# One transformer block on one core: the second norm, the second-half residuals and the shared-expert sums change engines

## The chip, the core and the metric

The kernel runs on one NeuronCore of one Trainium2 chip. The metric is the device time of one execution, in microseconds (us). Engines are named as the profile names them: PE multiplies matrices (PEld are its weight loads), DVE is the vector engine, ACT the scalar engine, POOL is GpSimd, SP issues the DMAs; "q" behind a name means the queue of that engine. All data are float32.

## The reference, cut to what matters

```python
# x: 4 batches of 512 tokens of width 512;  sa, ca, ga, sb, cb, gb: one row of 512 per batch
gb = (2 * (gb >= 0) - 1) * jnp.maximum(jnp.abs(gb), 0.25)      # ga likewise: never near zero
h = layernorm(x) * (1 + ca) + sa
x = x + ga * attention(h)                                      # 16 heads of 128, causal
h = layernorm(x) * (1 + cb) + sb                               # "the second norm"
x = x + gb * ffn(h)
# ffn(h) = shared(h) + sum over the top 2 of 8 experts of weight * expert(h)
# shared and expert are both silu(h @ wg.T) * (h @ wu.T) @ wd.T
```

Three pieces concern us: the second norm, the residual `x + gb * (shared + w1*y1 + w2*y2)`, and the shared expert's down projection.

## The kernel before

**Stages.** Attention runs over the four batches in turn, up to about 1270 us of the span; the second norm of a batch and its routing (`second_norm`, L943) are slipped into the attention of the following batch. For the last batch they are slipped into the first half of the shared expert instead. Then come: the shared expert for batches 0 and 1 ("half 1", about 1270 to 1389 us), 39 tiles of 128 routed tokens through their experts (about 1389 to 1709 us, results to `ys` in DRAM), and the shared expert for batches 2 and 3 ("half 2", from 1709 us), beside which the routed results of all 16 blocks of tokens are gathered and added by `combine`.

**Products.** Every large matrix product is done as seven products of quadrants in place of eight (`seven`, L510). A product fills one of three PSUM banks `w`, and DVE or ACT empties it; so PE can run two to three products ahead of DVE before it must wait. For this, sums and differences of the quadrants are needed: `hidden_sums` (L1274) makes four of them of the hidden values that feed the down projection of a batch, on DVE for the first batch of a half (n = 0), on POOL for the second (n = 1). `shared_down` (L1291) takes the seven products of the down projection and adds them, times gb, to the residual `xres`: DVE adds the two terms into `sy` and multiplies by gb (L1330 to L1333), POOL adds that to the residual (L1318). In the very last product (`last`, L1336) the two terms are multiplied by gb and added one by one, the last add on DVE.

**Second norm.** `normed` (L210): the statistics on DVE (L226, L227), a reciprocal root on ACT as Ln and Exp (L232, L233), then for each of four blocks of 128 tokens: `xh = src*rstd + less` on ACT (L251), times a row on DVE (L258), plus a row on POOL (L259). `less` is a small DVE operation right behind the Exp (L236). The four blocks are then transposed by PE (L267, tile `pln`) for the router. In the first norm (n = 1) one DVE operation (L242) does the subtraction and the scaling.

**Order.** The order on PE, DVE, ACT and SP is the order of the program text: generators that yield after each step are woven by hand (`weave`, `weave_at`), and an engine takes its instructions strictly in that order. POOL's order is left to a scheduler. `combine` (L1506) advances twice per block of tokens: ACT multiplies y1 by its weight, then DVE does `y2*w2 + y1` (L1511) and the product with gb (L1514), and POOL adds to the residual (L1515). The blocks of tokens come in the order of batches 0, 2, 3, 1; batches 0 and 1 are written out from `combine` (`finish`), batches 2 and 3 from `shared_down`.

Of the kernel before, what the change touches and what calls it, by code (L numbers as in the profile page):

```python
# [14 lines left out]
P = 128  # L15
# [16 lines left out]
FK = 3  # L32
# [16 lines left out]
def adaln_block_kernel(  # L49
# [160 lines left out]
    def normed(b, n, fine=(1,)):  # L210


        if n == 1:
            src = xh = late["first"]
        else:
            src = xres[b]
            xh = late["x"]
            rows = late["mod"]
            for t in range(NTB):
                nc.vector.tensor_mul(src[:, t, :], src[:, t, :], ga_bc)  # L220
                nc.gpsimd.tensor_add(src[:, t, :], src[:, t, :], xh[:, t, :])
                yield
        mv = small.tile([P, NTB, 2], F32, tag="mv", name=f"mv_{n}_{b}")
        for t in range(NTB):
            st = small.tile([P, 6], F32, tag="st", name=f"st_{n}_{b}_{t}")
            nc.vector.bn_stats(st, src[:, t, :])  # L226
            nc.vector.bn_aggr(mv[:, t, :], st)  # L227
            if t in fine:
                yield
        rstd = small.tile([P, NTB], F32, tag="rstd", name=f"rstd_{n}_{b}")  # L230
        nc.vector.tensor_scalar_add(rstd, mv[:, :, 1], EPS)
        nc.scalar.activation(rstd, rstd, AF.Ln)  # L232
        nc.scalar.activation(rstd, rstd, AF.Exp, scale=-0.5)  # L233
        if n == 2:
            less = small.tile([P, NTB], F32, tag="less", name=f"less_{n}_{b}")
            nc.vector.scalar_tensor_tensor(  # L236
                less, mv[:, :, 0], -1.0, rstd, op0=ALU.mult, op1=ALU.mult
            )
        yield
        for t in range(NTB):  # L240
            if n == 1:
                nc.vector.tensor_scalar(  # L242
                    xh[:, t, :],
                    src[:, t, :],
                    mv[:, t, 0:1],
                    rstd[:, t : t + 1],
                    op0=ALU.subtract,
                    op1=ALU.mult,
                )
            else:  # L250
                nc.scalar.activation(  # L251
                    xh[:, t, :],
                    src[:, t, :],
                    AF.Identity,
                    bias=less[:, t : t + 1],
                    scale=rstd[:, t : t + 1],
                )
                nc.vector.tensor_mul(xh[:, t, :], xh[:, t, :], rows[0])  # L258
                nc.gpsimd.tensor_add(xh[:, t, :], xh[:, t, :], rows[1])  # L259
            if t in fine:  # L260
                yield
        late[b] = xh
# [414 lines left out]
    def halves(a):  # L677
        return a.rearrange("p (t n) -> p t n", t=2)
# [592 lines left out]
            rows = slice(kh * FT, (kh + 1) * FT)  # L1271
            nc.vector.tensor_mul(hid[:FT, :, kh::2, 1, :], g[rows], u[rows])

    def hidden_sums(b, n, cs):  # L1274

        if n == 1:
            place = flat_of(h2s[b + 1])
            places = [place[:, q * FK * HW : (q + 1) * FK * HW] for q in range(3)]
        else:
            x1, x2 = wdn if b == 0 else [flat_of(w) for w in ws[:2]]  # L1280
            places = [x1[:, : FK * HW], x1[:, FK * HW : 2 * FK * HW], x2[:, : FK * HW]]
        s4, s5, s6 = (q.rearrange("p (c n) -> p c n", c=FK) for q in places)
        eng = nc.gpsimd if n else nc.vector
        a = hids[b][:, n]
        eng.tensor_add(s4[:, cs], a[:, 2, cs], a[:, 3, cs])
        eng.tensor_sub(s5[:, cs], s4[:, cs], a[:, 0, cs])
        eng.tensor_sub(a[:, 2, cs], a[:, 0, cs], a[:, 2, cs])
        eng.tensor_sub(s6[:, cs], a[:, 1, cs], s5[:, cs])
        return [a[:, q] for q in range(4)] + [s4, s5, s6]

    def shared_down(b, n, slots7):  # L1291

        bn = b + n

        def mm(i, dst):
            sa, sb_ = PROD[i]
            for t2 in range(2):
                for c in range(FK):
                    rows = FL if c == 1 else P
                    nc.tensor.matmul(  # L1300
                        dst[:, t2 * HW : (t2 + 1) * HW],
                        lhsT=slots7[sa][:rows, c, t2 * P : (t2 + 1) * P],
                        rhs=sdn[:rows, sb_, c, :],
                        start=(t2 == 0 and c == 0),
                        stop=(t2 == 1 and c == FK - 1),
                    )

        def gb(s):
            return gb_bc[:, bn, s * HW : (s + 1) * HW].unsqueeze(1).to_broadcast([P, 2, HW])

        def sy():
            return halves(work.tile([P, D], F32, tag="gy", name=f"sy_{bn}"))

        def into(r, s):
            return xres[bn][:, 2 * r : 2 * r + 2, s * HW : (s + 1) * HW]

        def done(r, s, y, eng=nc.gpsimd):
            eng.tensor_add(into(r, s), into(r, s), y)  # L1318
            if b >= half:
                nc.sync.dma_start(  # L1320
                    out=out[bn, r * HW : (r + 1) * HW, s * HW : (s + 1) * HW].rearrange(
                        "(t p) n -> p t n", p=P
                    ),
                    in_=into(r, s),
                )

        def add(p, u, r, s, less=False):
            y = sy()
            if less:
                nc.vector.tensor_sub(y, halves(u), halves(p))  # L1330
            else:
                nc.vector.tensor_add(y, halves(p), halves(u))
            nc.vector.tensor_mul(y, y, gb(s))  # L1333
            done(r, s, y)

        def last(p, u4):  # L1336
            if (b, n) != (half, 1):
                return add(p, u4, 0, 1)
            y = sy()
            nc.vector.tensor_mul(y, halves(p), gb(1))  # L1340
            done(0, 1, y, nc.vector)

        def less(p, u3):
            add(p, u3, 1, 0, True)
            if (b, n) == (half, 1):

                u4 = halves(places["p1"])
                nc.vector.tensor_mul(u4, u4, gb(1))
                nc.gpsimd.tensor_add(into(0, 1), into(0, 1), u4)

        places = {
            key: flat_of(h2s[b])[:, q * S : (q + 1) * S] for q, key in enumerate(("p1", "u2", "u3"))
        }
        yield from seven(
            f"d_{bn}",
            S,
            mm,
            {
                "p1": lambda o, p: nc.scalar.copy(o, p),
                "u2": lambda o, p, u: nc.vector.tensor_add(o, p, u),  # L1360
                "11": lambda p, p1: add(p, p1, 0, 0),
                "u3": lambda o, p, u: nc.vector.tensor_add(o, p, u),
                "22": lambda p, u3: add(p, u3, 1, 1),
                "u4": lambda o, p, u: nc.vector.tensor_add(o, p, u),
                "21": less,
                "12": last,
            },
            places,
        )

    def shared(b):

        for k in range(NSC):
            for n, _ in enumerate(in_order(shared_hidden(b, k))):
                if n == 0 and k > 0:
                    keep_hidden(b, k - 1)
                if n == 2 and k == NSC - 1:
                    hidden_sums(b, 0, slice(0, 2))
                yield
        keep_hidden(b, NSC - 1)  # L1380
        slots7 = hidden_sums(b, 0, slice(2, 3))
        more = hidden_sums(b, 1, slice(0, 3))
        yield from in_order(shared_down(b, 0, slots7))
        yield from in_order(shared_down(b, 1, more))

    NSEV = NSC * SEVEN
# [118 lines left out]

    def combine(n, bt):  # L1506
        b, t = divmod(bt, NTB)
        y1, y2 = (y_sb[n][:, k, :] for k in range(TOPK))
        nc.scalar.mul(y1, y1, cw[0][:, bt : bt + 1])
        yield  # L1510
        nc.vector.scalar_tensor_tensor(  # L1511
            y2, y2, cw[1][:, bt : bt + 1], y1, op0=ALU.mult, op1=ALU.add
        )
        nc.vector.tensor_mul(y2, y2, gb_bc[:, b, :])  # L1514
        nc.gpsimd.tensor_add(xres[b][:, t, :], xres[b][:, t, :], y2)  # L1515
        if b < half:
            finish(bt)

    with tc.manual_schedule(engines={ENG.PE, ENG.DVE, ENG.Activation, ENG.SP}):
        load_h2(0)  # L1520
# [52 lines left out]
            nc.sync.dma_start(out=xr[b], in_=xres[b].rearrange("p t d -> p (t d)"))  # L1573
        open_phase("tiles")
        turned = {0: tile_in(0, xts.pop(0))}
        flat, made = {}, {}
        for i in range(NT + 1):
            if i < NT:
                ht = tile_hidden(i, turned.pop(i))
# [13 lines left out]
            if i == 4:  # L1593
                load_h2(2)
                load_h2(3)
            if i == 8:
                most_of_b(nc.gpsimd, h2s[2])
                most_of_b(nc.gpsimd, h2s[3])
# [2 lines left out]
        open_phase("half2")  # L1601
        order = [bt for b in (0, 2, 3, 1) for bt in range(b * NTB, (b + 1) * NTB)]
        open_hidden(2)
        load_xr(2, moe, "xr0")
        load_xr(0, moe, "xr1")
        shared_tail(2)
        shared_tail(3)
# [134 lines left out]
```

## Time and profile before

| | |
|---|---|
| median of 3 runs | 1827.33 us (1825.96 to 1829.34) |
| the profiled execution: its own time | 1831.47 us |
| its span in the profile | 1829.8 us, 21973 instructions |
| PE busy | 1741.7 us (95%) |
| DVE busy | 884.8 us (48%) |
| POOL busy | 628.3 us (34%) |
| ACT busy | 562.7 us (31%) |
| mean granted PE clock | 0.983 |

The span is the stretch of the profile in which the engines work; the execution's own time holds 1.7 us more around it. Busy shares are means over stages that are very different: in the tile stage DVE is busy a fifth of the time, in half 2 nearly always. PE being "busy" includes matmuls that take twice as long because the granted clock is half, so the clock has to be read beside it.

### The profile page before, as it was taken

The page shows a single profiled execution, that of the slowest core. Times are in us where ns is not written, and L with a number is a line of the kernel's source. Part 1 is how long each engine was busy: PE and PEld are TensorE (multiplying, and loading weights), DVE is VectorE, ACT ScalarE, POOL GpSimd, SP SyncE. Part 2 cuts the span into 40 slices and gives each one's busy share as a digit, 9 for nine tenths or more (in the row PEclk, how much of TensorE's full clock was granted, in tenths as well). Part 3 has the DMA queues.
Part 4 walks back from the last instruction along what each step waited for, and adds up shares of the span by engine and source line. Part 5 has one row for each costly group of instructions (what it writes and reads, how often), then busy time and mean ns, then how long its engine had stood idle before and what let it go on. Part 6 is the DMA issues. An engine that isn't in the chain of part 4 may idle for free.

```text
span 1829.8 us, 21973 instructions
## 1 busy us (share of the span) xinstructions
PE 1741.7 (95%) x7637; PEld 1326.9 (73%) x7637; DVE 884.8 (48%) x1860; ACT 562.7 (31%) x1341; POOL 628.3 (34%) x726
## 2 busy tenths in 40 slices
PE   6999999997999999799999989999999999999997
PEld 4767778785887788678778767886786565565676
DVE  4554454455455555554654645444683211111497
ACT  1034443205445412534441354443310111111220
POOL 6344662305153312443331446435241100000475
PEclk9999999999999999899999989999999999999999
DMA  6569899545342243434243366436142656554442
GB/s 247 178 207 307 254 303 299 196 155 182 101 150 101 83 159 121 150 107 144 81 142 121 121 225 202 123 116 243 44 153 101 224 179 223 168 193 136 143 122 98
DMA packets 157838, 301.93 MB, mean 165 GB/s; under 512 B 19216, under 2 KB 97552, under 8 KB 151072
## 3 DMA queue, kind: packets, MB, share of 16 engines
q1 hardware_dynamic: 152608, 283.75, 46.3%
q0 software_dynamic: 5120, 16.78, 2.8%
q8 instruction: 61, 1.00, 0.2%
q14 instruction: 49, 0.40, 0.1%
HBM read 254.72 MB, written 97.03 MB: 192 GB/s over the span
## 4 chain that ended last, share of the span: by engine, by line
PE 79%; DVE 7%; POOL 5%; ACT 3%; DMA 3%; issue 2%; SPq 0%; POOLq 0%; ACTq 0%; DVEq 0%
PE w_v L687 10%; PE w_q L601 10%; PE w_o L724 9%; PE w_k L639 7%; PE ps L776 6%; PE po L818 6%; PE pyt L1469 5%; PE pgt L1442 5%; PE put L1442 5%; PE w_s L1227 4%; PE w_d L1300 4%; PE ppt L804 3%; ACT prob L794 1%; PE pxt L1429 1%; DMA xt<-xs 1%
## 5 line engine op out<-in xcount | busy, mean ns | idle before, releaser
L787 ACT ACTIVATE prob<-ps,nmax 128x128 f32<-128x128 f32 (+3 forms) x256 | 134.1, 524 | 371.7 <-DVE nmax L785 371.7
L639 PE MATMUL w_k<-h,wk 128*128 128x256 f32 x896 | 226.2, 391 | 4.8 <-DVE h L495 2.6
L724 PE MATMUL w_o<-wo,oS 128*128 128x256 f32 x896 | 208.9, 379 | 0.0
L687 PE MATMUL w_v<-wv,h 128*128 128x256 f32 x896 | 206.1, 379 | 2.0 <-DVE u_q L621 1.2
L601 PE MATMUL w_q<-h,wq 128*128 128x256 f32 x896 | 204.6, 383 | 1.3 <-DVE qT L627 1.3
L601 PEld LDWEIGHTS w_q<-h,wq 128*128 128x128 f32 x896 | 170.7, 192 | 28.0 <-issue 3.4
L639 PEld LDWEIGHTS w_k<-h,wk 128*128 128x128 f32 x896 | 168.3, 197 | 28.2 <-ACT p_k L651 4.8
L687 PEld LDWEIGHTS w_v<-wv,h 128*128 128x128 f32 x896 | 167.3, 190 | 23.9 <-DVE u_q L621 1.6
L724 PEld LDWEIGHTS w_o<-wo,oS 128*128 128x128 f32 x896 | 164.6, 190 | 21.3 <-issue 1.4
L776 PE MATMUL ps<-kT,qT 128*128 128x128 f32 (+3 forms) x512 | 177.0, 449 | 1.4 <-ACT prob L787 1.4
L818 PE MATMUL po<-probT,v 128*128 128x512 f32 (+3 forms) x512 | 153.5, 440 | 18.7 <-DVE probT L812 18.6
L818 PEld LDWEIGHTS po<-probT,v 128*128 128x128 f32 x512 | 96.1, 192 | 77.2 <-issue 30.3
L794 ACT ACTIVATE prob<-prob,rsum 128x128 f32<-128x128 f32 (+3 forms) x256 | 122.8, 551 | 55.7 <-DVE rsum L791 55.7
L804 PEld LDWEIGHTS ppt<-ident,prob 128*128 128x128 f32 x640 | 84.2, 144 | 74.4 <-issue 38.1
L1227 PE MATMUL w_s<-h2s,ws 128*128 128x256 f32 x560 | 126.1, 382 | 7.7 <-DVE wgu L1254 2.6
L737 POOL TENSOR_TENSOR xres<-xres,p_o 128x512 f32<-128x512 f32 x48 | 60.9, 1268 | 211.0 <-DVE xres L737 118.8
L785 DVE TENSOR_REDUCE nmax<-ps 128x1 f32<-128x128 f32 (+3 forms) x256 | 125.8, 491 | 8.8
L1227 PEld LDWEIGHTS w_s<-h2s,ws 128*128 128x128 f32 x560 | 104.7, 190 | 27.2 <-DVE wgu L1254 3.8
L804 PE MATMUL ppt<-ident,prob 128*128 128x128 f32 x640 | 108.9, 280 | 7.7 <-ACT prob L794 4.9
L783 DVE TENSOR_TENSOR ps<-ps,cmask 128x128 f32<-128x128 f32 x256 | 75.2, 294 | 70.6 <-PE ps L776 62.1
L1469 PE MATMUL pyt<-wdn,hTt 128*128 128x512 f32 (+1 forms) x234 | 107.0, 593 | 0.6 <-ACT yt L1477 0.6
L1452 DVE TENSOR_TENSOR ht<-tsg,put 128x352 f32<-128x352 f32 x39 | 20.3, 521 | 170.4 <-PE put L1442 165.6
(271 smaller groups left out, 2443.8 us busy)
## 6 DMA issues: line engine op xcount, KB each, us to landing
wgu<-in_wexp_dram SPq DMA_DIRECT2D x39, 1408.0 KB, 8.6
xs<-nothing SPq DMA_DIRECT2D x15, 2304.0 KB, 15.7
wdn<-in_wexp_dram SPq DMA_DIRECT2D x39, 768.0 KB, 4.4
wo<-sums_o SPq DMA_DIRECT2D x12, 1536.0 KB, 7.7
wq<-sums_q SPq DMA_DIRECT2D x24, 640.0 KB, 4.7
wk<-sums_k SPq DMA_DIRECT2D x24, 640.0 KB, 4.6
wv<-sums_v SPq DMA_DIRECT2D x12, 1280.0 KB, 7.1
xt<-xs SPq DMA_DIRECT2D x39, 256.0 KB, 2.9
```

Of the source, the lines that this page charges most:

```text
L601: nc.tensor.matmul(dst, lhsT=w[:, sa, c, :], rhs=h7[b][:, sb_, c, :], start=c == 0, stop=c == 1,)
L639: nc.tensor.matmul(dst, lhsT=w[:, sa, c, :], rhs=h7[b][:, sb_, c, :], start=c == 0, stop=c == 1,)
L687: nc.tensor.matmul(dst[:, t2 * HW : (t2 + 1) * HW], lhsT=h7[b][:, sb_, c, t2 * P : (t2 + 1) * P], rhs=w[:, sa, c, :], start=t2 == 0 and c ...
L724: nc.tensor.matmul(dst[:, t2 * HW : (t2 + 1) * HW], lhsT=oSs[hp][:, sa, t2 * P : (t2 + 1) * P], rhs=w[:, hp, sb_, :], start=t2 == 0 and hp ...
L776: nc.tensor.matmul(ps[:, :n], lhsT=qT[:, q0 : q0 + P], rhs=kT[:, u % 2, :n], start=True, stop=True,)
L787: nc.scalar.activation(blk, ps[:, :n], AF.Exp, bias=nmax, accum_out=rsum[:, i : i + 1])
L794: nc.scalar.mul(blk, blk, rsum[:, k : k + 1])
L804: nc.tensor.transpose(pt[:, at : at + P], prob[:, QO[i] + j * P : QO[i] + (j + 1) * P], ident,)
L818: nc.tensor.matmul(po[:, j * P :], lhsT=v()[:, j, u * DH : (u + 1) * DH], rhs=probT[:, KO[j] : KO[j] + (NTB - j) * P], start=(j == 0), sto ...
L1227: nc.tensor.matmul(dst[:, n * HW : (n + 1) * HW], lhsT=ws[k][:, sa, c, :], rhs=h2s[b + n][:, sb_, c, :], start=(n == 0 and c == 0), stop=( ...
L1442: nc.tensor.matmul(ps[:, :F], lhsT=xT[:, c, :], rhs=wgu[i % 2][:, at : at + F], start=(c == 0), stop=(c == NC - 1),)
L1469: nc.tensor.matmul(py, lhsT=hT_t[:fn, k, :], rhs=wdn[i % 2][:fn, k * D : (k + 1) * D], start=(k == 0), stop=(k == len(FCH) - 1),)
```

## The change

- **Second norm.** In batches 0, 1 and 2 the subtraction and scaling go from ACT to one DVE operation with two per-token scalars, as in the first norm; `less` is no longer made there. Only the last batch keeps the ACT form. The DVE product with a row and the POOL sum stay.
- **Residuals of batches 2 and 3.** During the tile stage, from tile 6 on, `divided` loads the residual of batch 2 (this load was at the start of half 2), makes 1/gb for the two batches in eight pieces of 128 columns on DVE, and multiplies the eight residual blocks by it on POOL, one step per tile. `combine` for these batches is then two DVE operations `x = y*w + x`; `shared_down` adds both terms into the residual and multiplies the finished block by gb, all on DVE.
- **Residuals of batches 0 and 1** in `shared_down`: the add into the residual goes from POOL to DVE.
- **hidden_sums** is a generator, always on DVE. The first two thirds for n = 0 are taken one operation after each of four products of the fifth piece (before: all four together); those for n = 1 one after each of four products of the first batch's down projection (before: POOL).

```diff
@@ normed
+        idle = n == 2 and b == B - 1
+        if idle:
             less = small.tile(...)
...
         for t in range(NTB):
-            if n == 1:
+            if not idle:
                 nc.vector.tensor_scalar(xh[:, t, :], src[:, t, :], mv[:, t, 0:1], rstd[:, t : t + 1], ...)
             else:
                 nc.scalar.activation(xh[:, t, :], src[:, t, :], AF.Identity, bias=less..., scale=rstd...)
+            if n == 2:
                 nc.vector.tensor_mul(xh[:, t, :], xh[:, t, :], rows[0])
                 nc.gpsimd.tensor_add(xh[:, t, :], xh[:, t, :], rows[1])
@@ hidden_sums
-        eng = nc.gpsimd if n else nc.vector
-        eng.tensor_add(s4[:, cs], a[:, 2, cs], a[:, 3, cs])
-        eng.tensor_sub(s5[:, cs], s4[:, cs], a[:, 0, cs])
-        eng.tensor_sub(a[:, 2, cs], a[:, 0, cs], a[:, 2, cs])
-        eng.tensor_sub(s6[:, cs], a[:, 1, cs], s5[:, cs])
+    def hidden_sums(slots7, cs):
+        a11, a12, a21, a22, s4, s5, s6 = (a[:, cs] for a in slots7)
+        nc.vector.tensor_add(s4, a21, a22)
+        yield
+        nc.vector.tensor_sub(s5, s4, a11)
+        yield
+        nc.vector.tensor_sub(a21, a11, a21)
+        yield
+        nc.vector.tensor_sub(s6, a12, s5)
+        yield
@@ shared_down
+        def add(r, s, *terms, sub=None):
             if b >= half:
+                if sub is not None:
+                    nc.vector.tensor_sub(into(r, s), into(r, s), halves(sub))
+                for a in terms:
+                    nc.vector.tensor_add(into(r, s), into(r, s), halves(a))
+                nc.vector.tensor_mul(into(r, s), into(r, s), gb(s))
                 nc.sync.dma_start(out=..., in_=into(r, s))
+                return
             y = sy()
             ...                                   # y = the two terms, as before
             nc.vector.tensor_mul(y, y, gb(s))
-            done(r, s, y)                         # POOL: into += y
+            nc.vector.tensor_add(into(r, s), into(r, s), y)
+        def u4(o, p, u2):
+            nc.vector.tensor_add(o, p, u2)
+            if b >= half:
+                nc.vector.tensor_add(into(0, 1), into(0, 1), halves(o))
         def last(p, u4):
-            if (b, n) != (half, 1):
-                return add(p, u4, 0, 1)
-            ...
+            add(0, 1, p, *(() if b >= half else (u4,)))
@@ shared
+        sums7 = hidden_sums(slots7, slice(0, 2))
-                if n == 2 and k == NSC - 1:
-                    hidden_sums(b, 0, slice(0, 2))
+                if 0 < n < 5 and k == NSC - 1:
+                    next(sums7)
...
-        more = hidden_sums(b, 1, slice(0, 3))
-        yield from in_order(shared_down(b, 0, slots7))
+        for n, _ in enumerate(in_order(shared_down(b, 0, slots7))):
+            if 1 < n < 6:
+                next(sums7)                       # the sums of batch b + 1
+            yield
@@ combine
+        if b >= half:
+            nc.vector.scalar_tensor_tensor(x_t, y1, w1, x_t, op0=ALU.mult, op1=ALU.add)
+            yield
+            nc.vector.scalar_tensor_tensor(x_t, y2, w2, x_t, op0=ALU.mult, op1=ALU.add)
+            return
...
+    def divided():
+        load_xr(2, moe, "xr0")
+        rgb = phase[-1].tile([P, 2, D], F32, tag="rgb", bufs=1, name="rgb")
+        for n in range(2):
+            for c in range(NC):
+                cols = slice(c * P, (c + 1) * P)
+                nc.vector.reciprocal(rgb[:, n, cols], gb_bc[:, half + n, cols])
+                yield
+        for b in range(half, B):
+            for t in range(NTB):
+                nc.gpsimd.tensor_mul(xres[b][:, t, :], xres[b][:, t, :], rgb[:, b - half, :])
+                yield
@@ tile loop
+            if i >= 6:
+                next(ready, None)
...
-        load_xr(2, moe, "xr0")
```

## The prediction, made before the changed kernel was run

> **What bounds the kernel now.** I read the chain that ended last, then the list of what PE waited for, then the timeline and the windows around the longest waits. The chain first (shares of the span by engine), then PE's waits (total us, times, longest):
>
> ```profile
> PE 79%; DVE 7%; POOL 5%; ACT 3%; DMA 3%; issue 2%; SPq 0%; POOLq 0%; ACTq 0%; DVEq 0%
> ```
> ```profile
> PE po L818 <- DVE probT L812: 18.6, 8, 4.0
> PE pln L267 <- POOL xh L259: 15.2, 6, 4.3
> ...
> PE w_s L1227 <- DVE wgu L1254: 2.6, 1, 2.6
> ```
>
> PE is the bound, so only its waits and its clock are worth anything. The two large waits lie in one place: the second norm of batches 0, 1 and 2. Asked by window (425:475, 735:785, 1040:1090 us), PE waits 3.7, 3.7, 4.0 us for `probT` and 5.2, 5.1, 4.8 us for `xh`. The timeline of batch 0 (start, length, engine, line, what, and in brackets the idle time before it and who ended it):
>
> ```profile
> 441.36 0.17 DVE L236 SCALAR_TENSOR_TENSOR less<-mv,rstd 128x4 f32<-128x4 f32 x1 [1.99 <-ACT rstd L233]
> ...
> 442.97 1.11 PE L818 MATMUL po<-probT,v 128*128 128x256 f32 x4 [3.70 <-DVE probT L812]
> ...
> 448.45 0.73 POOL L486 TENSOR_TENSOR oS<-oS 128x256 f32<-128x256 f32 x1 [0.34 <-ACT oS L825]
> ...
> 449.11 1.82 DVE L258 TENSOR_TENSOR xh<-xh,rows 128x512 f32<-128x512 f32 x2 [3.26 <-ACT xh L251]
> ...
> 452.27 2.48 POOL L259 TENSOR_TENSOR xh<-xh,rows 128x512 f32<-128x512 f32 x2
> ...
> 453.59 0.33 PE L267 MATMUL pln<-ident,xh 128*128 128x128 f32 x1 [4.33 <-POOL xh L259]
> ```
>
> DVE stands 1.99 us at `less` because ACT makes the root behind two table loads; `probT` is behind `less`, so PE stands 3.70 us. Then blocks 2 and 3 of `xh` wait for ACT, and on POOL they stand behind four `oS` sums (448.45 to 452.27). After such waits the clock is half (columns: PE, PEld, DVE, ACT, POOL busy, then PEclk, DMA share, GB/s):
>
> ```profile
> 455.00:460.00 5.00, 5.00 (x17) 3.82 (x17) 1.28 (x3) 1.82 (x5) 1.12 (x2) 0.50 0.47 135
> ```
>
> In windows of 1 us the half clock, with PE working, lasts from 454.8 to 464.0, 762.1 to 767.8 and 1067.9 to 1071.6 us: 18.6 us at half speed, 9.3 us lost.
>
> The second place is half 2. There DVE is the late one:
>
> ```profile
> 1760.00:1780.00 20.00, 16.82 (x73) 13.25 (x73) 18.89 (x23) 3.89 (x7) 14.26 (x13) 1.00 0.36 105
> ```
> ```profile
> 1769.18 2.46 DVE L1268 TENSOR_TENSOR hid<-wgu,wgu 128x1024 f32<-128x1024 f32 x1 [0.70 <-ACT wgu L1244]
> 1769.27 1.27 POOL L1515 TENSOR_TENSOR xres<-xres,y_sb 128x512 f32<-128x512 f32 x1
> ...
> 1774.36 2.15 DVE L1285 TENSOR_TENSOR ws<-hid 128x512 f32<-128x512 f32 x1
> 1774.68 1.27 POOL L1515 TENSOR_TENSOR xres<-xres,wdn 128x512 f32<-128x512 f32 x1
> ```
>
> The same L1268 takes 1.23 us where POOL is still (1783.52 us), and L1285 takes 0.68 us in half 1: DVE pays for POOL's add. From 1761.2 to 1781.1 us PE does 72 matmuls, 15.6 us at its 0.2167 us each; with 0.6 us at the first `w_d` it loses 4.9 us to DVE.
>
> **What the Trainium skill says.** "SBUF — State Buffer", section "SBUF: two separate sides": the port pair that DVE and POOL share is an exclusive lock, held for a whole instruction, taken by DVE for two SBUF inputs or a two-port mode. The lines above agree (1.23 becomes 2.46 beside a POOL add of 1.27). "TensorE: Matmul & The Clock Gate", section "What's actually happening": the clock falls to half after about one idle window of 3.4 us, and windows run freely. The trace agrees: three of three waits of 3.7 us or more halved it, the 2.6 us wait in half 2 did not. "VectorE: DVE Perf Modes", section "First, the fixed hardware budget": the reciprocal repeats 8 times per element. No long reciprocal is in this trace (only 128x4, 0.17 us); my estimate from that page is 128 x 8 / 0.96 GHz = 1.1 us a piece.
>
> **The change, part by part.**
>
> *Second norm, three batches.* Removed: 3 `less`, 12 ACT operations of 0.80 us. Added: 12 DVE operations like L242, 0.54 us alone, 0.95 to 1.48 beside POOL. With `less` gone, DVE runs mask, maximum and `probT` from 439.4 on, so `probT` is ready 2.0 us sooner and PE's 3.7 us wait becomes 1.7. In the built order, POOL now does all four `xh` adds ahead of the `oS` sums. DVE's and POOL's work there takes turns at the lock: from the root (441.36), one `u_k` add 0.73 + 4 x 1.27 (POOL) + 4 x (0.54 + 0.69) (DVE) = 10.7 us, so the last block is ready at 452.1, not 454.8: **2.7 us sooner, 8.1 us over three batches**. The first 2 us, at `probT`, is not counted again: PE then waits here. Late next: PE reaches `pln` at about 447.9 and stands until 452.1 with one transpose between. Almost idle windows of 3.4 us fit in, depending on their phase; I put the chance of the half clock at 0.6 per batch and its cost at 3.2 us (6.4 us at half), so two batches of three have it. Where it stays full, POOL is next: the `oS` sums (3.8 us) now stand before the `kT` and `p_k` adds (L669, L671), which DVE's L654 and `probT` behind it wait for; I charge 0.8 us. Sum: 8.1 + 9.3 - 2 x 3.2 - 0.8 = **10.2 us gained**. Bounds: half clock in all three, 8.1 + 9.3 - 9.6 = 7.8; full in all three, 8.1 + 9.3 - 2.4 = 15.0. If the lock overlapped better than in strict turns, up to 3 us a batch more.
>
> *Half 1.* DVE gets 8 adds of 0.69 (L1318 moved) and 4 sums of 768 elements, 0.95 us each (0.16 + 1.02 per 1000 from 0.42 and 0.68 for 256 and 512): +9.3 us inside the 36.6 us of `w_d` products, where DVE idles about half, and POOL's disturbance goes (three L1286 to L1288 at 1.99 become 0.43, -4.7). PE hides it, except at the end: the first tile's `xT` (L1433) stands behind the last block, one add more: +0.65 us. The spread sums let DVE use a gap (0.58 us at 1343.9), which shortens the 0.8 us wait of the first `w_d`: -0.6. Together **0**.
>
> *Tile stage.* The 1 MB load goes into SP's queue behind tile 6 (about 1448 us); the DMA share from 1446 to 1458 is 0.14 to 0.35 and the next real weight load starts at 1459.7, so nothing stands behind it. Eight reciprocals of 1.1 us and eight POOL products of 1.27 lie beside PE, in tiles where DVE has over 4 us between its steps. **0**; if a reciprocal took over 4 us, up to 8 x 0.5; a late `xt` would cost at most the 0.7 us that the two h2 loads cost now. No gain here: PE is 99.5% busy.
>
> *Half 2.* DVE loses nothing per `combine` of batches 2 and 3: two operations of 0.745 for 0.745 + 0.69, +0.4 us over eight; ACT loses eight products of 0.71. `shared_down`: 7 more DVE operations of 0.69 = 4.8; four sums of 0.95 = 3.8. **+9.0 us of DVE work.** Against it, POOL's 8 + 8 adds and 4 sums go. In DVE's groups from 1706 to 1819 us the time above the undisturbed length is L1268 3.2, L1511 3.6, L1333 2.2, L1272 1.3, L1514 0.9, L1285 to L1288 6.2: 17.4 us, of which I take 14 to vanish (four adds of batch 0, four of batch 1 and the gathers remain). Per seven products PE needs 12.1 us; DVE had about 13.2 and will have 10.6. The waits of 4.9 us fall to about 0.8: **4.1 us gained**, bounds 0 (DVE as late as now) and 4.9. In the down products DVE has 17.5 us of work per 18.2 us, within the banks' slack.
>
> *The end.* Now POOL's L1318 and L1349 hold the last residual until 1820.2; DVE's add, the last `combine` and POOL's add follow to 1823.6, 5.3 us behind PE's last product. After: DVE add, product, the two `combine` operations, POOL add: 0.05 + 4 x 0.7 + 1.3 plus a lag of 0.5 = 4.7. **0.6 us gained.** The first residual DMA no longer waits for POOL; SP's order is else the same.
>
> Sum: 10.2 + 0 + 0 + 4.1 + 0.6 = 14.9 us: from the profiled 1831.5 to 1816.6. That execution is 4.1 us above the median of the runs; the gain is in waits that every run has, so **1827.3 - 14.9 = 1812 us**.
>
> **The rivals.**
> 1. *The clock stays full in all three norms, or the lock costs less*: 15.0 to 22 + 4.7, so 1801 to 1808 us. For: no single wait above 2.2 us is left. Against: 4 us with almost no matmul. Chance 0.25.
> 2. *The lock eats the norm's gain*: with DVE operations at 1.48 and POOL's at 1.75, the turns last as long as the ACT chain did (13.4 us); what is left is half 2 and a little clock, 4.7 to 8 us: 1819 to 1823. Chance 0.13.
> 3. *Slower: DVE becomes the bound of half 2.* It was busy 18.9 of 20 us; if POOL's remaining adds and gathers disturb it as much as all do now, the 9.0 us come straight onto PE, and with rival 2 in the norm the time is 1836. It decides from more than 12.1 us of DVE work per seven products. Against: the disturbing adds are named above and go. Chance 0.05.
> 4. *Nothing moves*: the waits only change their names (POOL's `oS` and `k` adds hold PE as long): about 1826, within 0.2%. Chance 0.04.
>
> **How the numbers follow.** The forecast, 1807 to 1818 alone, has 0.53; rivals 0.25, 0.13, 0.05, 0.04. The range 1800 to 1822 takes in the first two. 0.2% is 3.7 us, about what a measurement here can tell from no change: faster 0.91, same 0.04, slower 0.05.
>
> **What would show it.** Right: no `less` wait on DVE and PE's `probT` waits at about 1.7 us; `pln` waits below 2.5 us; half clock behind them shorter or gone; L1268 at 1.23 us in half 2; no `w_s` wait above 1 us from 1740 us on. Wrong: `pln` waits still above 4 us; new L243 operations above 1.2 us; PE waits for DVE in the `w_d` products; a wait for `xt` near tile 8.

## The result: 1807.5 us, and the profile after

The changed kernel takes **1807.49 us** (median of 4 runs, 1806.03 to 1808.81) against 1827.40 us before (4 runs): ratio 0.989, 95% interval 0.9873 to 0.9907. The profiled execution took 1807.06 us, with a span of 1805.3 us and a mean PE clock of 0.990. In the changed code the lines of `normed` stand two lower (L812 is now L814, L258 is L260, L259 is L261, L242 is L243), L1268 is L1270, and the two operations of the new `combine` are L1525 and L1527.

The chain that ended last, and then PE's waits over the whole span (total us, times, longest):

```profile
PE 79%; DVE 8%; POOL 4%; ACT 4%; DMA 2%; issue 2%; SPq 0%; POOLq 0%; ACTq 0%; DVEq 0%
```
```profile
PE po L820 <- DVE probT L814: 13.0, 9, 2.7
PE ppt L806 <- ACT prob L796: 12.1, 17, 2.1
...
PE pln L269 <- POOL xh L261: 2.7, 3, 0.9
...
PE pgt L1456 <- DVE xT L1447: 2.4, 1, 2.4
```

PE is still the bound. Its wait for `xh` fell from 15.2 to 2.7 us and that for `probT` from 18.6 to 13.0, but part came back under another name: PE now waits 12.1 us for `prob` (4.9 us in the trace before). Here `prob` is a block of softmax weights, `rsum` the reciprocal of its row sums, `ppt` its transposes on PE, `probT` their copy, and `po` the product of `probT` with the values. The wait for `wgu` in half 2 has gone from the list.

Where the time went, from the starts of PE's groups in the two traces (`pst` is the first product of each half of the shared expert, `pxt` the transposes of a tile's tokens and `xT` their copy, `pgt` the tile's first expert product, `w_d` a down product):

| stretch | before | after | gain | predicted |
|---|---|---|---|---|
| to the first `pst` (attention and three norms) | 1269.9 | 1251.0 | 18.9 | 10.2 |
| to the first `pxt` (half 1) | 118.7 | 118.1 | 0.6 | 0.6 |
| to the first `pgt` (`xT` of the first tile) | 2.4 | 3.0 | -0.6 | -0.65 |
| to the first `pst` of half 2 (tile stage) | 318.0 | 318.9 | -0.9 | 0 |
| to the last `w_d` product (half 2) | 108.9 | 103.4 | 5.5 | 4.1 |
| to the end of the span | 11.9 | 10.9 | 1.0 | 0.6 |

They add up to the 24.5 us between the two spans. That is 4.6 us more than lies between the medians: the traced execution of the kernel before was a slow one (1831.47 us), and the experiments show where.

**The norm.** The timeline of batch 0 (start, length, engine, line, what, and the idle time before it with who ended it):

```profile
441.16 0.92 PE L820 MATMUL po<-probT,v 128*128 128x256 f32 x4 [1.54 <-DVE probT L814]
...
441.72 0.55 DVE L243 TENSOR_SCALAR xh<-xres,mv,rstd 128x512 f32<-128x512 f32 x1 [0.61 <-ACT rstd L233]
...
443.53 1.44 POOL L261 TENSOR_TENSOR xh<-xh,rows 128x512 f32<-128x512 f32 x1
443.89 1.63 DVE L260 TENSOR_TENSOR xh<-xh,rows 128x512 f32<-128x512 f32 x1
445.44 0.17 DVE L793 RECIPROCAL rsum<-rsum 128x4 f32<-128x4 f32 x1
...
445.60 1.57 POOL L261 TENSOR_TENSOR xh<-xh,rows 128x512 f32<-128x512 f32 x1 [0.63 <-DVE rsum L793]
445.64 1.92 ACT L796 ACTIVATE prob<-prob,rsum 128x128 f32<-128x128 f32 x4 [2.93 <-DVE rsum L793]
...
446.10 0.72 PE L806 MATMUL ppt<-ident,prob 128*128 128x128 f32 x2 [2.14 <-ACT prob L796]
...
447.80 1.50 POOL L261 TENSOR_TENSOR xh<-xh,rows 128x512 f32<-128x512 f32 x1 [0.63 <-DVE xh L260]
...
449.93 1.26 POOL L261 TENSOR_TENSOR xh<-xh,rows 128x512 f32<-128x512 f32 x1 [0.63 <-DVE xh L260]
...
451.25 0.33 PE L269 MATMUL pln<-ident,xh 128*128 128x128 f32 x1 [0.89 <-POOL xh L261]
```

From the root (441.68) to the last `xh` (451.19) it is 9.5 us; before it was 13.4 us (441.32 to 454.75). Adds on POOL and products on DVE (L260 at 1.63 us, 0.69 alone) take turns. The small reciprocal of `rsum` stands on DVE behind two blocks of `xh`, ACT's `prob` waits for it, and so PE waits 2.14 us at `ppt`. The wait of 5.2 us for `xh` has become one of 2.1 us for `prob` and one of 0.9 us for `xh`. The clock follows (width, PE busy, PEclk, DMA share, GB/s):

```profile
446.00:448.00 2.00, 1.51 (x5) 0.68 0.00 0
448.00:450.00 2.00, 2.00 (x7) 0.50 0.25 58
450.00:452.00 2.00, 1.11 (x6) 0.96 0.98 174
452.00:454.00 2.00, 2.00 (x16) 1.00 0.79 154
```

It is half for 3.4 us here, and full from the moment that the real work resumes; before, it was half until 464.

**Half 2 and the end.** The window answering to the one shown of before (PE, PEld, DVE, ACT, POOL busy, PEclk, DMA share, GB/s), and the products on DVE that read `wgu`:

```profile
1751.00:1771.00 20.00, 20.00 (x94) 17.54 (x93) 15.97 (x25) 3.08 (x5) 2.84 (x3) 1.00 0.38 119
```
```profile
L1270 DVE TENSOR_TENSOR hid<-wgu,wgu x4: 1225/1574/2465, 1712.2 to 1759.9; 128x1024 f32<-128x1024 f32 x4
```

PE never stops, DVE is no longer full (16.0 of 20 us), and POOL is nearly still. L1270's minimum, median and maximum are 1.225, 1.574 and 2.465 us: two of four (1.92 and 2.46 us) still run beside POOL's adds of batch 0. The prediction's reckoning had kept these adds, but its sign, 1.23 us in half 2, came true for the other two alone.

**Between half 1 and the tiles** a new loss stands. The copy of the first tile's block keeps PE waiting 2.40 us, and eight products of 2.63 us in the trace before take 4.14 us:

```profile
1372.07 4.14 PE L1456 MATMUL pgt<-wgu,xT 128*128 128x352 f32 x8 [2.40 <-DVE xT L1447]
```

### The profile page after: what moved, and what is told of

Same layout as the page of the kernel before. It is cut to its first block, busy times and chain, and to the rows that moved or that the text cites. A ratio compares the mean times of both kernels' runs of the same rounds, so it can differ in the third digit from the quotient of the medians.

```text
span 1805.3 us, 21946 instructions
## 1 busy us (share of the span) xinstructions
PE 1732.3 (96%) x7637; PEld 1319.4 (73%) x7637; DVE 901.6 (50%) x1900; ACT 549.2 (30%) x1321; POOL 587.9 (33%) x702
## 4 chain that ended last, share of the span: by engine, by line
PE 79%; DVE 8%; POOL 4%; ACT 4%; DMA 2%; issue 2%; SPq 0%; POOLq 0%; ACTq 0%; DVEq 0%
PE w_v L689 10%; PE w_q L603 10%; PE w_o L726 10%; PE w_k L641 7%; PE ps L778 6%; PE po L820 5%; PE pyt L1483 5%; PE pgt L1456 5%; PE put L1456 5%; PE w_s L1229 5%; PE w_d L1310 3%; PE ppt L806 3%; ACT prob L796 1%; DVE xh L260 1%; PE pxt L1443 1%
## 5 line engine op out<-in xcount | busy, mean ns | idle before, releaser
L820 PE MATMUL po<-probT,v 128*128 128x512 f32 (+3 forms) x512 | 151.7, 436 | 13.1 <-DVE probT L814 13.0
L739 POOL TENSOR_TENSOR xres<-xres,p_o 128x512 f32<-128x512 f32 x48 | 60.9, 1270 | 212.6 <-DVE xres L739 118.7
L806 PE MATMUL ppt<-ident,prob 128*128 128x128 f32 x640 | 109.9, 280 | 15.0 <-ACT prob L796 12.1
L785 DVE TENSOR_TENSOR ps<-ps,cmask 128x128 f32<-128x128 f32 x256 | 75.1, 293 | 59.7 <-PE ps L778 47.9
L1456 PE MATMUL pgt<-wgu,xT 128*128 128x352 f32 x312 | 100.4, 465 | 2.5 <-DVE xT L1447 2.4
```

The costliest lines, as they stand in the source:

```text
L806: nc.tensor.transpose(pt[:, at : at + P], prob[:, QO[i] + j * P : QO[i] + (j + 1) * P], ident,)
L820: nc.tensor.matmul(po[:, j * P :], lhsT=v()[:, j, u * DH : (u + 1) * DH], rhs=probT[:, KO[j] : KO[j] + (NTB - j) * P], start=(j == 0), sto ...
L1456: nc.tensor.matmul(ps[:, :F], lhsT=xT[:, c, :], rhs=wgu[i % 2][:, at : at + F], start=(c == 0), stop=(c == NC - 1),)
```

## The experiments

Theory: the gain is mostly the norm (its wait and the clock behind it), and half 2 gives the rest. Rivals: the gain is DVE's relief in half 2; or the norm's first wait or the clock is worth nothing by itself. "Before" in the comparisons is the kernel before in the same set of runs: 1827.93 us (e1 to e4), 1826.69 us (e5 to e8), 1826.19 us (e9 to e11).

### e1: the norm alone, and e2: all but the norm

e1 is the kernel before with the norm's part of the diff; e2 is the kernel after with one condition changed:

```diff
-        idle = n == 2 and b == B - 1
+        idle = n == 2
```

> The kernel before with the change of the second norm alone (batches 0 to 2 on DVE). Theory (the norm's wait and the half clock behind it): the start of half 1 comes 19 us earlier in the profile than in that of the kernel before, as it does in the changed kernel, and nothing changes behind it; 13 to 16 us faster in the median. Rival (half 2 gives a good part): under 8 us.

> The changed kernel with the second norm back on ACT in all batches, all else kept. Theory: 4 to 6 us faster than before, all of it after the start of half 2 (5.5 us there, 0.9 at the end), with the norm's waits of 3.7 and 5.2 us back. Rival (the parts depend on each other): no gain left, or more than 10 us.

Measured: e1 **1813.66 us**, ratio 0.9918 (0.9898 to 0.9938), 14.3 us faster. e2 **1822.76 us**, ratio 0.9976 (0.9960 to 0.9993), 5.2 us faster. Together 19.5 us of the change's 19.9: the parts add, as far as intervals some 6 to 7 us wide can tell, and the norm is nearly three quarters of the gain. The rival that looked to half 2 for it is out. In e1's trace half 1 starts 22.6 us earlier than in the trace before, not 19 as expected; the stretches behind it are within 0.6 us of those before. The traced execution (1808.88 us) is the quickest of e1's six.

### e3: only the sums of hid on DVE, and e11: only the residuals

e3 is the kernel before with `hidden_slots`, `hidden_sums` and `shared` of the kernel after. e11 is e2 with those three as they were before.

> The kernel before with hidden_sums on DVE, one operation after each product, and nothing else; POOL keeps its adds. Theory (POOL's adds at the shared port make DVE late): the 2.6 us wait at the bunched sums goes, the rest stays, since L1268 and L1511 are still disturbed: 1.5 to 3 us faster. Rival (bunching was the whole cause): 4 to 5 us faster, no PE wait left in half 2.

> The kernel after with the second norm and the sums of hid as before: only the residuals divided by gb, the combine of two operations and the shared adds in place are left. Theory that the parts of half 2 add: e2 (all but the norm, 4.4 us) less e3 (the sums, 1 to 2.4 us) leaves 2 to 3.5 us, 1823 to 1825. Rival that the sums had to leave GpSimd first: under 1 us, 1826 to 1827.

Measured: e3 **1827.04 us**, ratio 0.9987 (0.9975 to 1.0000). e11 **1823.86 us**, ratio 0.9985 (0.9977 to 0.9993), 2.3 us faster. e3 is below what its theory and its rival expected. In their traces half 2, from its first `pst` to its last `w_d` product, takes 109.3 us in e3 and 103.4 us in e11. It takes 103.4 us in all six traces with the new residuals (after, e2, e6, e7, e8, e11) and 108.9 to 110.2 us in the seven without. So in half 2 the residuals give all of it and the sums nothing. The wait of 2.6 us for `wgu` is gone in e3, but PE's waits there are 0.7, 0.6 and 0.5 us for `wgu` and 0.8 us for `hid`; e11 has none for DVE. The window of e11 shows a PE that never stops with the sums still on POOL:

```profile
1749.00:1769.00 20.00, 20.00 (x94) 17.60 (x94) 17.59 (x26) 3.69 (x6) 8.77 (x9) 1.00 0.46 130
```

The sums' place is half 1: from its first `pst` to the first `pxt` it takes 118.0 or 118.1 us in the six traces with the new sums and 118.7 to 119.1 in the seven without.

### e4: the norm's first wait alone

The kernel before, with `less` made on POOL, so that DVE no longer stands at it while ACT makes the root:

```diff
-            nc.vector.scalar_tensor_tensor(less, mv[:, :, 0], -1.0, rstd, ...)
+            nc.gpsimd.tensor_scalar_mul(less, mv[:, :, 0], -1.0)
+            nc.gpsimd.tensor_mul(less, less, rstd)
```

> The kernel before with only the small product less made on POOL (two small operations), so that DVE no longer stands behind the root; the norm stays on ACT. Theory (the first wait is given back at the second): PE's probT wait falls from 3.7 to about 1.7 us per batch, the wait for xh grows by as much, and the time changes by under 2 us. Rival (each wait counts for itself): 6 us faster.

Measured: **1824.10 us**, ratio 0.9972 (0.9961 to 0.9984), 3.8 us faster. PE's waits in batch 0 (425 to 480 us):

```profile
PE pln L266 <- POOL xh L258: 3.9, 2, 3.1
PE ppt L803 <- ACT prob L793: 1.9, 3, 1.5
PE po L817 <- DVE probT L811: 1.5, 1, 1.5
```

The `probT` wait fell from 3.7 to 1.5 us and 1.6 us came back at `prob`; but the whole chain moved too. ACT starts the first `xh` 0.9 us behind the root in place of 2.2 us, since the softmax step that stood ahead of it came sooner as well, and the last `xh` is there 12.2 us after the root (13.4 before). The wait for `xh` fell from 5.2 to 3.9 us and did not grow. The theory that this wait is only given back fell; the rival's 6 us did not come in full.

### e5 and e9: the wait kept, the clock restored

PE is given products to do in the wait for `xh`, into a bank that is overwritten; e5 takes 16 and 6 of them, e9 takes 9 and 3:

```diff
         for t in range(NTB):
+            if n == 2 and c == 0 and b < B - 1 and t >= 2:
+                for _ in range(16 if t == 2 else 6):
+                    nc.tensor.matmul(pt[:, t * P : 4 * P], lhsT=ident,
+                        rhs=late["mod"][0][:, : (4 - t) * P], start=True, stop=True)
             nc.tensor.transpose(...)
```

> The kernel before, with TensorE kept busy in its last wait of each norm: 16 extra products (identity by a row of 256) ahead of the first transpose that waits 4.3 us for xh, and 6 of 128 columns ahead of the next, in batches 0 to 2. They write a bank that the transposes overwrite, so the result is the same; nothing else moves. Theory: half the loss in this norm is the clock, not the wait. TensorE comes back after the 4.3 us wait at half clock for 10 to 11 us (454 to 465 in batch 0), some 3 us lost in each of three batches once the work that is not matmul-bound is taken off: 1825 becomes 1815 to 1820, with the wait itself still there and the clock at 1.00 after it. Rival: the half clock costs nothing beyond the wait, and the time is the same or some tenths longer.

> The filler of e5 cut to the size of the wait: 9 products of 256 columns (0.44 us each in e5, 4.0 us against a wait of 4.3 us) and 3 of 128 (0.25 us each, 0.75 against 0.89 us), so that the path is not lengthened as e5's was by 3.35 us in each of three batches. Theory: e5's 10 us of overshoot cost only 3.3 us, so some 7 us came back from the clock; with the overshoot gone the time is 6 to 8 us below the kernel before, 1819 to 1821. Rival: e5 was only a smaller overshoot than reckoned and the clock is worth nothing: 1826 to 1828.

e5: **1830.03 us**, ratio 1.0016 (1.0007 to 1.0024), slower. The filler was too long, as its trace shows (one product of the program is two instructions there):

```profile
448.73 7.07 PE L269 MATMUL pln<-rows,ident 128*128 128x256 f32 x32
...
455.75 1.50 PE L269 MATMUL pln<-rows,ident 128*128 128x128 f32 x12
```

8.6 us of products stand where PE waited 5.2 us, 3.35 us too many in each of three batches. That this cost 3.3 us and not 10 already speaks for the clock. e9, with the filler cut to the wait, took **1820.50 us**, ratio 0.9968 (0.9957 to 0.9980): **5.7 us faster with the waiting for `xh` only filled, not shortened**: in batch 0 the first transpose behind it starts 12.3 us after the root, as in the kernel before. The rival (the clock is worth nothing) is out.

### What half clock costs in each trace

From windows of 1 us over 425 to 490, 735 to 800 and 1030 to 1095 us, the missing share of the clock, summed over all windows, and over them weighted by PE's busy time:

| | before | e4 | e9 | e10 | after | e6 | e1 | e8 |
|---|---|---|---|---|---|---|---|---|
| missing clock, us | 18.7 | 15.3 | 6.8 | 20.4 | 6.8 | 10.2 | 3.4 | 3.4 |
| of it with PE busy | 15.7 | 8.7 | 5.9 | 15.6 | 5.7 | 8.7 | 3.0 | 3.4 |

The first row counts in steps of 1.7 us: 11, 9, 4, 12, 4, 6, 2 and 2 of them. One step is 3.4 us at half clock.

Each column is one execution, and they are not alike: those of e1, e4 and e10 are the quickest of their runs, those of before and e9 the slowest. The kernels after, e1 and e7 share the norm's code and lack 6.8, 3.4 and 10.2 us. The table can't rank versions that lie close together. For e9 all runs agree with it: the median of their mean granted clocks is 0.9915 against 0.986 for the kernel before, some 10 us of clock. For e4 they don't: 0.985 against 0.985, so its gain in the median is not shown to be clock.

### e6: POOL taken out of the norm, and e10: the same in the old form

Both put the add of `xh` on DVE in batches 0 to 2, e6 in the kernel after, e10 in the kernel before:

```diff
-                nc.gpsimd.tensor_add(xh[:, t, :], xh[:, t, :], rows[1])
+                (nc.gpsimd if b == B - 1 else nc.vector).tensor_add(xh[:, t, :], xh[:, t, :], rows[1])
```

> The kernel after, with the add of the second norm (xh + row) on VectorE too in batches 0 to 2, so that all twelve operations of a norm stand on one engine and GpSimd takes no turn at the lock. Theory of the lock: in the kernel after the four adds on GpSimd (1.3 to 1.6 us) and the three later products on VectorE (1.6 us) run in turns, 9.5 us from the root to the last xh; on VectorE alone it is 8 operations of 512 elements at 0.71 us (the adds, products) and 4 at 0.37 us (2.2 us for the four scalings with their first wait), some 7.5 us. The last xh is 1.5 to 2 us sooner in each batch, 1802 to 1806. Rival: the softmax steps queued on VectorE behind the adds come later by what GpSimd no longer takes, and the time is the same or up to 3 us longer.

> The kernel before, the scaling left on ScalarE, with only the add of the second norm on VectorE in batches 0 to 2. Then the last two adds no longer stand behind the four sums of oS (448.5 to 452.3 in batch 0) on GpSimd. Theory that ScalarE's order is the bound: the last two scalings stand behind prob and oS on ScalarE, and the first two adds on VectorE (1.5 us) put off the reciprocal of rsum that prob waits for, so the last xh comes 0 to 2 us sooner: 0 to 4 us in all, 1823 to 1827. Rival that GpSimd's order is the bound: 2.5 us sooner in each batch and less of the half clock behind it, 1815 to 1819.

e6: **1803.89 us**, ratio to the kernel before 0.9878 (0.9863 to 0.9893), 3.6 us under the median of the kernel after. The kernel after was measured in another set of runs, and the intervals of the two ratios overlap (0.9873 to 0.9907 for the kernel after). The products with the row on DVE take 0.69 us again (1.63 beside POOL), the last `xh` comes 8.6 us after the root, and in batch 0 PE has no wait for `xh` left. So the turns with POOL were real. What they cost is less clear: of the 4.0 us between the two spans 2.3 lie ahead of half 1 and 1.7 in the tile stage, which e6 leaves alone.

e10: **1832.27 us**, ratio 1.0035 (1.0022 to 1.0047), slower, and outside what either theory said. Its timeline, in batch 0:

```profile
443.66 0.69 DVE L259 TENSOR_TENSOR xh<-xh,rows 128x512 f32<-128x512 f32 x1
444.26 0.17 DVE L793 RECIPROCAL rsum<-rsum 128x4 f32<-128x4 f32 x1
444.47 1.92 ACT L796 ACTIVATE prob<-prob,rsum 128x128 f32<-128x128 f32 x4 [2.19 <-DVE rsum L793]
446.29 0.67 ACT L827 ACTIVATE oS<-po,bvT 128x512 f32<-128x512 f32 x1
446.86 1.51 ACT L251 ACTIVATE xh<-xres,less,rstd 128x512 f32<-128x512 f32 x2
...
450.68 1.10 DVE L259 TENSOR_TENSOR xh<-xh,rows 128x512 f32<-128x512 f32 x1
451.70 0.28 DVE L785 TENSOR_TENSOR ps<-ps,cmask 128x128 f32<-128x128 f32 x1
```

With ACT still scaling, two of the adds put off `rsum`, ACT waits 2.19 us for it, and its second pair of scalings comes behind that. The last `xh` is 13.2 us after the root (13.4 before), so nothing is won, and the next mask step (L785) stands 13.1 us after the root in place of 9.5. In this trace the order on ACT holds the last `xh`, as the first theory had it; the gain of 0 to 4 us that this theory expected did not come. The cause of the loss stays open: the profiled execution is the quickest of e10's five (1827.75 us) and doesn't show 6 us. The mean clock of the five executions is 0.983 to 0.985 against a median of 0.986 for the kernel before, so some of it may be clock.

### e7: the first tile's copy on ACT

The kernel after with one copy moved:

```diff
-        nc.vector.tensor_copy(xT.rearrange("p c s -> p (c s)"), pt)
+        (nc.scalar.copy if i == 0 else nc.vector.tensor_copy)(xT.rearrange("p c s -> p (c s)"), pt)
```

> The kernel after, with the copy of the first tile's turned block (xT) on ScalarE instead of VectorE, where it stands behind hid and the residual of half 1 and keeps TensorE waiting 2.4 us, with half the clock for 3.4 us after it. Theory: the wait falls to under 1 us and the half clock goes, 2 to 3 us in all, 1804 to 1806. Rival: only the wait shrinks, or ScalarE's copy is late for another reason, and the gain is under 1.5 us.

Measured: **1806.14 us**, ratio to the kernel before 0.9891 (0.9878 to 0.9904), 1.4 us under the kernel after, where the intervals overlap. By the time alone its rival (under 1.5 us) is not refuted. At the place itself the trace shows:

```profile
1371.41 2.63 PE L1458 MATMUL pgt<-wgu,xT 128*128 128x352 f32 x8 [0.67 <-ACT xT L1447]
```

The wait is 0.67 us for 2.40, and the eight products take 2.63 us for 4.14. From the first `pst` to the last it is 443.6 us for 446.4, 2.8 us less; the whole does not show it clearly, and in this execution 10.2 us of clock are missing in the norms against 6.8. Only the shorter wait is the copy's doing for certain. Whether half clock follows the wait differs between executions: in e6 the same wait of 2.40 us is followed by full clock, and in e9, with the copy as in the kernel before, a wait of 1.74 us by half clock:

```profile
1369.68 2.63 PE L1456 MATMUL pgt<-wgu,xT 128*128 128x352 f32 x8 [2.40 <-DVE xT L1447]
```
```profile
1382.90 4.33 PE L1451 MATMUL pgt<-wgu,xT 128*128 128x352 f32 x8 [1.74 <-DVE xT L1442]
```

### e8: the norm in two operations, a faster version

The kernel after with e7's copy, and for batches 0 to 2 in place of three operations on two engines:

```diff
+            if n == 2 and not idle:
+                nc.vector.scalar_tensor_tensor(xh[:, t, :], src[:, t, :], mv[:, t, 0:1], rows[0],
+                    op0=ALU.subtract, op1=ALU.mult)
+                nc.vector.scalar_tensor_tensor(xh[:, t, :], xh[:, t, :], rstd[:, t : t + 1], rows[1],
+                    op0=ALU.mult, op1=ALU.add)
```

> The kernel after, with the ScalarE copy of e7 and the second norm of batches 0 to 2 as two operations of VectorE for each tile, (x - mean) * row and (that) * rstd + row, with nothing on GpSimd: four pairs of about 0.75 us are 6.0 us against the 9.5 us from the root to the last xh in the kernel after, and the first of a pair does not wait for the root. Theory that the norm's chain still sets TensorE's wait: 3 to 4 us sooner in each of three batches at the xh wait, of which some 1.5 us are left there now (pln waits 0.9 us, ppt 2.1 us and po 1.5 us behind the same operations), so 2 to 5 us, and 2 to 3 us of the copy: 1798 to 1803. Rival: the waits left are of the softmax and not of the norm, and it is e7's time.

Measured: **1796.55 us** (1796.01 to 1799.57), ratio to the kernel before 0.9839 (0.9825 to 0.9853), the fastest of all, 10.9 us under the median of the kernel after, 9.6 under e7 in the same set of runs, and better than expected. In batch 0:

```profile
439.35 0.74 DVE L243 SCALAR_TENSOR_TENSOR xh<-xres,mv,rows 128x512 f32<-128x512 f32 x1
...
439.80 0.20 ACT L233 ACTIVATE rstd<-rstd 128x4 f32<-128x4 f32 x1
...
444.95 0.75 DVE L247 SCALAR_TENSOR_TENSOR xh<-xh,rstd,rows 128x512 f32<-128x512 f32 x1
...
446.75 1.06 PE L281 MATMUL pln<-ident,xh 128*128 128x128 f32 x4
```

The first operation starts before the root is there, the last `xh` is ready 5.7 us after it, and PE takes its four transposes without a wait.

## Why the prediction was right, and where it was not

The forecast was 1812 us within 1800 to 1822. The result, 1807.5 us, lies in that range, at the lower edge of the forecast's own 1807 to 1818 and the upper edge of rival 1's 1801 to 1808. The places and the mechanism were right, the sizes mostly too small. That the result lies in the forecast's own range is partly luck: in the traces the gain was 24.5 us against a sum of 14.9, 9.6 us more, and 4.6 of these are absent from the medians because the traced execution of before was slow.

- **The norm: mis-sized, 10.2 us predicted, 14.3 measured alone (e1; 11.3 to 18.6 by its interval).** Three terms of the sum moved.
  - *"The first 2 us, at `probT`, is not counted again"* was a wrong step. e4 takes away this wait alone and gains 3.8 us, about what is missing. The last `xh` comes 1.2 us sooner after the root as well.
  - *The clock: 9.3 us lost before, 6.4 us still lost after.* The second number was nearly right (5.7 us with PE busy). The first counted only the stretches behind the last wait; some 6 us of the 15.7 stood behind the `probT` wait (443 to 447, 750 to 755 and 1056 to 1062 us) and were left out. The prediction counted three of three waits of 3.7 us or more that halved the clock; with those for `probT` they are six of six. So in the traces 10.0 us of missing clock went in place of 2.9.
  - *Waits: 8.1 less 0.8 us.* In the windows of the three norms, waits at `po`, `pln` and `ppt` fell from 27.1 to 15.9 us, so 11.2. The turns at the lock gave 3.9 us a batch, not 2.7 (9.5 us from root to last `xh`, not 10.7): POOL's adds start 2.07, 2.20 and 2.13 us apart, where the sum has 1.27 + 0.54 + 0.69 = 2.50 us for a block, so the turns were not strict.
  - *Late next.* PE did not stand at `pln` from 447.9 to 452.1; `prob`, behind `rsum` on DVE, held it first. This was not named.
  - Waits and clock together, 21.2 us, are more than the 18.9 us by which the stretch shortened between the traces. They overlap, and how the missing 4 us of the median split among these terms is not shown.
- **Half 1 and the first tile**: 0.6 and -0.6 us as worked out. The longer `xT` wait (2.4 us for 1.7) was followed by half clock in the traced execution, 1.5 us on eight products. The prediction had only the 0.65 us of the wait. By e6 and e9 the half clock is chance and not the longer wait's sure price.
- **Tile stage: 0.** Apart from that half clock it held: PE waits once for a late `xt`, 0.6 us, where it waited twice before, 1.1 us. A reciprocal takes less than the estimate of 1.1 us (from the list of groups: count | busy, mean ns | idle before it):

```profile
L1543 DVE RECIPROCAL rgb<-gb_bc 128x128 f32<-128x128 f32 x8 | 7.5, 943 | 0.0
```

- **Half 2: 4.1 predicted, 5.5 in the trace.** DVE's lateness went entirely, 0.8 us was not left over. The sums' move, counted in the same reckoning, was not needed: e11 has the whole 5.5 us. From runs the residuals alone give 2.3 us, the sums alone 0.9, both in e2 5.2; the intervals are too wide to say that more than the sum is there. In the traces of e2 and e11 the first tile's wait and the tile stage take 1.7 to 2.0 us more than before, which hides part of half 2's gain.
- **The end**: 1.0 us for 0.6.
- **"The gain is in waits that every run has"** was wrong in part. The traces differ by 24.5 us and the medians by 19.9. The old norm in e2, e3 and e11 reached the first `pst` at 1268.7, 1268.3 and 1263.9 us (1269.9 before), with 17.0, 18.7 and 17.0 us of clock missing in the norms. How much clock is lost differs between executions of the same code, and the traced one of before was a dear one.
- **The rivals.** Rival 1 came as close as the forecast, and half of it came true: the lock did cost less, but the clock was still half for a while in all three norms of the traced execution. Rival 2 (the lock eats the gain) is refuted by e1, rival 3 by the windows of half 2, rival 4 by the result.

## What to carry to other kernels

Price a wait of the busiest engine together with the clock behind it: filling a wait without shortening it was worth 5.7 us here. Take the clock's part from many executions, since one trace shows one draw of it. When a chain of small operations holds that engine, look first at what else stands in the same queue behind a wait (here `probT` behind `less`), and then for a form with fewer operations on one engine: two fused operations on DVE beat three on two engines by 3.8 us of chain in each batch, and three on DVE alone (e6) by 2.9 us. An operation moved off a queue helps only if the next queue in the chain is not late as well, as e10 shows.

## What the runs showed of the hardware that was not expected

- **Half clock came without an idle stretch of 3.4 us.** The Trainium skill, "TensorE: Matmul & The Clock Gate", section "What's actually happening", puts the fall at about one idle window of 3.4 us, windows running freely. Length and free running agree: in each of the thirteen traces of this case the clock changes only on a grid of 3.413 us, whose phase against the start of the span lies anywhere from 0.2 to 3.2 us. But the window need not be idle. In the kernel after, PE had no idle stretch above 2.14 us between 442 and 447 us in batch 0; it was busy 1.2 us of the window from 443.3 to 446.7, and the clock was half from 446.7 to 450.1.
- **How busy a window must be.** The windows of all thirteen traces, from 10 us into the span on, give a count (PE busy by the profile's account). Of the windows at full clock, all 82 with PE busy under 42% were followed by half clock, 25 of 102 between 42 and 60%, and 2 of 6520 above. Of the windows at half clock all 37 with PE busy under 75% were followed by another. So it matters how a wait lies on the grid. The wait of 2.6 us in half 2 of the kernel before fell on two windows, 51 and 58% busy, and did not halve the clock. The 2.40 us for `xT` did in the kernel after (one window, 39%) and did not in e6 (two, 65% each).
- A DVE product of 512 elements took 1.63 us beside POOL's adds and 0.69 us alone, and a POOL add 1.44 to 1.57 us beside DVE's work and 1.26 alone: sharing cost both.
- A reciprocal of 128x128 on DVE took 0.943 us for 128 columns, where a product of 512 columns takes 0.69 us. The prediction's estimate of 1.1 us from eight repeats was a little dear.
